# Softmax of the first cross attention: eight short exponentials on ScalarE for half of the heads

## The chip, the cores and the metric

The kernel runs on one core of a Trainium2 chip. A core has five engines with instruction queues of their own: TensorE (PE; its weight loads are listed apart as PEld), VectorE (DVE), ScalarE (ACT), GpSimd (POOL) and SyncE (SP), which issues DMAs. Each queue is worked in order: an instruction that waits holds up everything behind it on its engine. The metric is the device time of one execution in microseconds (us). The kernel before took 1720.57 us, the median of nine runs between 1716.8 and 1725.27.

## The reference

A decoder of two layers on x (16 sequences of 256 rows of 256 numbers) and a context of 77 rows per sequence, all in float32. Each layer adds an attention, a cross attention and a feed-forward part, with a layer normalization ahead of each. Layer 0 has a linear attention, the cross attention that this change touches, and a mixture of 16 experts; layer 1 has a latent attention, another cross attention and a feed-forward part with simulated quantization. The part that matters:

```python
q = jnp.einsum('bfd,dnh->bfnh', query_input, wq)        # 16 heads of 16
k = jnp.einsum('btd,dnh->btnh', source_input, wk)       # 77 context rows
v = jnp.einsum('btd,dnh->btnh', source_input, wv)
q = q * HEAD_DIM ** (-0.5)
logits = jnp.einsum('btnh,bfnh->bnft', k, q) + bias
weights = jax.nn.softmax(logits, axis=-1)
attn = jnp.einsum('bnft,btnh->bfnh', weights, v)
return jnp.einsum('bfnh,nhd->bfd', attn, wo)
```

For every row of x and every one of 16 heads there is a softmax over 77 numbers: subtract the largest, exponentiate, divide by the sum.

## The kernel before

The 4096 rows of x lie in SBUF as 32 tiles of 128 rows (`E.xs`). The stages follow each other: linear attention (`l0_attention`), cross attention (`l0_cross`), experts (`l0_experts`), layer 1's two attentions (`l1_tokens`), layer 1's feed-forward (`l1_ffn`).

`l0_cross` (line 1009) goes over the 32 tiles. For tile i, `scores(i)` (line 1032) multiplies queries and keys into PSUM in two halves (m = 0 and 1) of eight heads each, `ps_sc`. For each half a DVE step adds the mask and writes `lx_s` (128 rows, 8 heads, 77 numbers: 616 per row); DVE takes the maximum of each head, `lx_mx`; POOL subtracts it (`lx_s<-lx_s,lx_mx`); ACT exponentiates all 616 in place; DVE sums each head into `lx_sum`. After both halves DVE takes the reciprocal `lx_rec` of the 16 sums and POOL spreads it to `lx_wide`. `weighted(i)` (line 1071) turns `lx_s` with 16 transposes on PE into PSUM (`ps_pt`), from where four copies bring it to `lx_sT`; PE turns `lx_wide` and multiplies the weights with the values (`ps_rec`); a copy `lx_rT` and a DVE product `lx_aT` apply the reciprocal; PE multiplies with the output weights, and DVE adds the result to x. `scores(i + 1)` is recorded ahead of `weighted(i)`, so the softmax of one tile has the products of the tile before beside it. PSUM banks for transposes, projections and router products come from one ring of three (`pp`), `ps_rec` has one buffer, `lx_s` four.

Beside this loop run, for every four tiles, the queries and keys of a later group (`hT`, `lx_q`, `lx_k`, `ps_v`), and the router of the experts for the group before (`R.take`: normalization `la_rstd` on POOL, `la_shift` on DVE, `rh` on ACT, transposes `ps_rt`, products `ps_logit`, then `rt_...` steps on DVE, and eight indirect DMAs per group from POOL that scatter rows into `moe_x`). For the last tiles the router goes in smaller steps, tile by tile.

The order on each engine isn't that of the program. `planned` (class `Plan`, line 54 on) records all operations of a stage with estimated durations and lays them out one by one: among operations that can begin within 150 ns of the earliest it takes the one with the lowest rank (place in the program, shifted by `urgent`). The instructions are then issued in order of their planned begin; the profile gives nearly all of them line 363, where `Call.issue` calls the engine. A PSUM copy recorded with `copy` may go to DVE or ACT; the planner takes the one that would end it sooner. So another cost at one place changes the order, and the engine of copies, elsewhere in the stage.

Of the kernel before, what the change touches and what calls it, by code (L numbers as in the profile page):

```python
# [21 lines left out]
AF = mybir.ActivationFunctionType  # L22
ALU = mybir.AluOpType
AX = mybir.AxisListType
# [984 lines left out]
def l0_cross(E, W, X, raw, made):  # L1009
# [9 lines left out]
    with ExitStack() as ctx, planned(E) as nc:  # L1019
# [12 lines left out]
        def scores(i):  # L1032

            G, a = X.ready[i // 4], i % 4
            cols = slice(a * P, (a + 1) * P)
            sums = w3.tile([P, KD, 8], F32, name="lx_sum", tag="lx_sum")
            filled = []
            for m in range(KD):

                sc = psc.tile([P, 2, 512], F32, name="ps_sc", tag="sc")  # L1040
                with nc.together():
                    for r in range(2):
                        rows = slice(64 * r, 64 * r + 64)
                        nc.tensor.matmul(
                            sc[:, r, : Q * S2], G.qT[m][rows, cols],
                            X.keyed[i // 4][m][rows, i % 4 // 2, :, :].rearrange("p n k -> p (n k)"),
                            start=True, stop=True,
                        )
                filled.append(sc)
            weights = []  # L1050
            for m in range(KD):
                s = w3.tile([P, 8, S2], F32, name="lx_s", tag="lx_s", bufs=4)
                nc.vector.tensor_tensor(
                    s.rearrange("p (r n) k -> p r n k", r=2),
                    filled[m][:, :, : Q * S2].rearrange("p r (n k) -> p r n k", n=Q),
                    G.bias[:, a, :].unsqueeze(1).unsqueeze(1).to_broadcast([P, 2, Q, S2]),
                    ALU.add,
                )
                mx = w3.tile([P, 8, 1], F32, name="lx_mx", tag="lx_mx")
                nc.vector.tensor_reduce(mx, s, AX.X, ALU.max)  # L1060
                nc.gpsimd.tensor_tensor(s, s, mx.to_broadcast([P, 8, S2]), ALU.subtract)
                nc.scalar.activation(s, s, AF.Exp)
                nc.vector.tensor_reduce(sums[:, m, :], s, AX.X, ALU.add)
                weights.append(s)
            rec = w3.tile([P, H0], F32, name="lx_rec", tag="lx_rec")
            nc.vector.reciprocal(rec, sums.rearrange("p m n -> p (m n)"))
            wide = w3.tile([P, H0, DH0], F32, name="lx_wide", tag="lx_wide")
            nc.gpsimd.tensor_copy(wide, rec.unsqueeze(2).to_broadcast([P, H0, DH0]))
            return weights, wide
# [52 lines left out]
        def step(side, n=1):  # L1122
            for _ in range(n):
                next(side, None)

        held = scores(0)
        f = kv = route = last = none
        for i in range(NT):
# [6 lines left out]
            if i + 1 < NT:  # L1135
                held = scores(i + 1)
                mark = len(nc.ops) - 1
# [956 lines left out]
```

## Time and profile before

| what | us |
|---|---|
| median of nine runs | 1720.57 |
| profiled execution | 1722.94 |
| its span, first to last instruction | 1721.2 |
| PE busy (9268 matmuls) | 1588.3 |
| DVE busy | 1129.6 |
| ACT busy | 736.2 |
| POOL busy | 498.4 |
| first and last start of the masking step `lx_s<-ps_sc` | 275.1 and 549.2 |

The profile is of one execution. Its times count from the first instruction. "Busy" is the time in which an engine had at least one instruction under way; rows give the mean of one instruction, and instructions of a queue can overlap by some tens of nanoseconds, so the distance between two starts can be smaller than a duration. An arrow to the left names the tile or the step that something came from or waited for. The granted clock is TensorE's, as a share of full speed.

### The profile page before, as it was taken

To read this page: it belongs to the slowest core of one execution; us is meant where nothing else is said; L and a number is where in the kernel's file an instruction comes from. 1 tells how busy PE (TensorE), PEld (TensorE's weight loads), DVE (VectorE), ACT (ScalarE), POOL (GpSimd) and SP (SyncE) were. 2 spreads that over 40 slices of the span, in tenths; PEclk is the share of its full clock that TensorE was granted. 3 is DMA by queue.
4 is the path that set the end of the run, shared out by engine and by line. 5 is a ranking of instruction groups with operands and counts; after the bars stand their busy time and mean duration, and the time that the engine had idled before them with its cause. 6 is when DMAs were issued, how large, how long until landed. Compare 5 with 4: busy or idle time off the path is not lost.

```text
span 1721.2 us, 24227 instructions
## 1 busy us (share of the span) xinstructions
PE 1588.3 (92%) x9268; PEld 1067.4 (62%) x9268; DVE 1129.6 (66%) x2212; ACT 736.2 (43%) x1551; POOL 498.4 (29%) x570
## 2 busy tenths in 40 slices
PE   6999999999996799999997999999999689999799
PEld 3666666666664667777775666666666444433387
DVE  7988886999996343211123888966767543899941
ACT  4343324556563211111112654554555343667850
POOL 5332113576666200000003787433343100000000
PEclk9999999999997699999998999999999899999899
DMA  6000008211011154343322121000000000001111
GB/s 187 1 1 1 2 1 244 78 43 33 29 36 38 51 173 129 111 138 125 123 83 68 45 65 47 4 1 1 1 1 1 1 1 0 25 25 61 37 50 49
DMA packets 75231, 90.76 MB, mean 53 GB/s; under 512 B 11934, under 2 KB 64886, under 8 KB 75114
## 3 DMA queue, kind: packets, MB, share of 16 engines
q1 hardware_dynamic: 68970, 72.64, 13.1%
q0 software_dynamic: 6144, 16.57, 3.0%
q8 instruction: 73, 1.20, 0.3%
q14 instruction: 44, 0.36, 0.1%
HBM read 52.70 MB, written 36.70 MB: 52 GB/s over the span
## 4 chain that ended last, share of the span: by engine, by line
PE 59%; DVE 25%; issue 6%; ACT 5%; DMA 2%; POOL 1%; SPq 1%; POOLq 0%; ACTq 0%; DVEq 0%
PE ps_y L363 7%; PE ps_h L363 7%; PE ps_pr L363 7%; PE ps_av L363 5%; PE ps_out L486 5%; PE ps_gate L486 5%; PE ps_sc L363 4%; PE ps_pt L363 4%; PE ps_v L363 2%; PE ps_po L363 2%; DVE sa_top L363 2%; DVE lx_s L363 2%; PE ps_rec L363 2%; DVE x L363 2%; DVE ff_g L1957 2%
## 5 line engine op out<-in xcount | busy, mean ns | idle before, releaser
L363 DVE COPY ex_y<-ps_y 128x256 f32<-128x256 f32 x80 | 33.7, 424 | 218.7 <-PE ps_y L363 218.7
L363 POOL DMA_INDIRECT ex_yg<-moe_y,slot x64 | 63.4, 991 | 347.2 <-issue 345.7
L363 POOL TENSOR_TENSOR sa_e<-sa_e,sa_rec 128x1024 f32<-128x1024 f32 x64 | 121.5, 1905 | 121.2 <-PE ps_pt L363 71.4
L486 PE MATMUL ps_up<-ff_x,ffn_up 128*128 128x512 f32 x336 | 148.7, 601 | 7.1 <-DVE ff_pu L1828 4.3
L363 ACT ACTIVATE sa_e<-ps_sc,sa_top 128x256 f32<-128x256 f32 x256 | 118.2, 485 | 72.4 <-DVE sa_top L363 70.1
L363 PE MATMUL ps_y<-w,ex_h 128*128 128x256 f32 x640 | 143.2, 383 | 3.8 <-DVE ex_y L363 3.8
L363 PE MATMUL ps_h<-ex_xT,w 128*128 128x320 f32 x512 | 143.9, 439 | 0.5 <-ACT ex_h L363 0.5
L363 PEld LDWEIGHTS ps_y<-w,ex_h 128*128 128x128 f32 x640 | 122.5, 192 | 23.6 <-DVE ex_y L363 5.0
L363 ACT ACTIVATE ex_h<-ps_h 128x640 f32<-128x640 f32 x64 | 45.0, 704 | 186.9 <-PE ps_h L363 186.9
L363 PEld LDWEIGHTS ps_h<-ex_xT,w 128*128 128x128 f32 x512 | 96.9, 192 | 40.6 <-issue 1.2
L486 PEld LDWEIGHTS ps_up<-ff_x,ffn_up 128*128 128x128 f32 x336 | 63.6, 192 | 92.1 <-issue 74.5
L486 PE MATMUL ps_out<-ffn_down,ff_g 128*128 128x256 f32 x384 | 85.8, 388 | 10.3 <-issue 10.3
L486 PE MATMUL ps_gate<-ff_x,ffn_gate 128*128 128x512 f32 x192 | 84.2, 601 | 6.5 <-DVE ff_x L1930 6.5
L486 PEld LDWEIGHTS ps_out<-ffn_down,ff_g 128*128 128x128 f32 x384 | 74.8, 195 | 21.8 <-issue 11.1
L363 DVE TENSOR_REDUCE sa_top<-ps_sc 128x4 f32<-128x1024 f32 x64 | 76.3, 1214 | 16.4 <-PE ps_sc L363 15.9
L363 POOL TENSOR_TENSOR lx_s<-lx_s,lx_mx 128x616 f32<-128x616 f32 x64 | 77.8, 1221 | 25.4 <-DVE lx_mx L363 14.7
L363 DVE TENSOR_TENSOR la_at<-ps_sc,la_tri 128x1024 f32<-128x1024 f32 x64 | 75.8, 1214 | 8.6 <-PE ps_sc L363 8.6
L363 PE MATMUL ps_pt<-ident,lx_s 128*77 128x128 f32 x512 | 77.5, 295 | 0.4 <-ACT lx_sT L363 0.4
L363 ACT COPY lx_sT<-ps_pt 77x512 f32<-77x512 f32 x113 | 62.0, 582 | 30.5 <-PE ps_pt L363 29.4
L363 POOL DMA_INDIRECT moe_x<-rh,slot x64 | 64.7, 1011 | 31.1 <-issue 10.5
L363 PE MATMUL ps_pt<-ident,sa_e 128*128 128x128 f32 x512 | 67.3, 283 | 6.1 <-DVE x L363 1.9
L363 PE MATMUL ps_sc<-sa_latT,sa_q 64*128 64x256 f32 x512 | 70.1, 400 | 2.3 <-ACT sa_e L363 2.3
(289 smaller groups left out, 3377.7 us busy)
## 6 DMA issues: line engine op xcount, KB each, us to landing
w<-in_L_ffn_w SPq DMA_DIRECT2D x32, 512.0 KB, 3.8
moe_x<-rt_zero SPq DMA_DIRECT2D x16, 640.0 KB, 8.2
ex_xg<-moe_x SPq DMA_DIRECT2D x15, 640.0 KB, 6.7
moe_y<-ex_y SPq DMA_DIRECT2D x15, 640.0 KB, 5.7
x<-in_x SPq DMA_DIRECT2D x32, 128.0 KB, 3.3
out_x<-x SPq DMA_DIRECT2D x32, 128.0 KB, 1.7
ff_u<-ff_c SPq DMA_DIRECT2D x6, 512.0 KB, 2.9
ff_c<-ff_u SPq DMA_DIRECT2D x6, 512.0 KB, 3.2
```

Source lines behind the costliest of these rows:

```text
L363: made = getattr(getattr(self.nc, self.engine), self.method)(*self.args, **self.kwargs)
L486: E.nc.tensor.matmul(ps, a, b, start=n == 0, stop=n == last)
L1957: nc.vector.scalar_tensor_tensor(gp, low16(gq, I16), sg16, low16(sig, U16), ALU.mult, ALU.mult)
```

## The change

For the second half of each tile (m = 1) the maximum is taken with its sign turned, and instead of one subtraction on POOL, one exponential on ACT and one sum on DVE there are eight activations on ACT, one per head of 77 numbers. Each adds the negative maximum as its bias, exponentiates in place, and gives the head's sum into `lx_sum` through the activation's accumulator. The first half (m = 0) is as before. `weights.append(s)` moves up so that both halves reach it.

```diff
                 mx = w3.tile([P, 8, 1], F32, name="lx_mx", tag="lx_mx")
+                weights.append(s)
+
+
+                if m:
+                    nc.vector.tensor_reduce(mx, s, AX.X, ALU.max, negate=True)
+                    for n in range(8):
+                        nc.scalar.activation(
+                            s[:, n, :], s[:, n, :], AF.Exp, bias=mx[:, n, :],
+                            accum_out=sums[:, m, n : n + 1],
+                        )
+                    continue
                 nc.vector.tensor_reduce(mx, s, AX.X, ALU.max)
                 nc.gpsimd.tensor_tensor(s, s, mx.to_broadcast([P, 8, S2]), ALU.subtract)
                 nc.scalar.activation(s, s, AF.Exp)
                 nc.vector.tensor_reduce(sums[:, m, :], s, AX.X, ALU.add)
-                weights.append(s)
```

The planner's estimate for an activation is 170 ns and 0.73 ns per number, and 92 ns more with an accumulator (line 347).

## The prediction

> **What bounds the kernel now.** I read the page first: TensorE (PE) is busy 92% of the span, VectorE (DVE) 66%, ScalarE (ACT) 43%, GpSimd (POOL) 29%. The changed stage, cross attention of layer 0, shows in the instruction rows as the stretch from 275 to about 580 us (first and last `lx_s` work). So the second view is the table of windows over that stretch. Columns: window length, then busy us and instruction count of PE, PE's weight loads, DVE, ACT and POOL, then granted clock, DMA share, GB/s.
>
> ```profile
> 345.00:381.00 36.00, 34.00 (x311) 24.22 (x310) 34.21 (x93) 21.19 (x41) 24.37 (x31) 1.00 0.13 42
> 381.00:416.00 35.00, 33.59 (x306) 23.74 (x305) 33.20 (x91) 21.28 (x41) 22.51 (x30) 1.00 0.10 33
> 416.00:452.00 36.00, 34.59 (x313) 24.51 (x312) 34.20 (x94) 21.28 (x41) 23.50 (x30) 1.00 0.12 38
> 452.00:487.00 35.00, 33.53 (x306) 23.81 (x306) 33.20 (x90) 21.27 (x41) 22.54 (x30) 1.00 0.10 32
> 487.00:523.00 36.00, 33.33 (x306) 23.29 (x304) 33.09 (x83) 20.80 (x39) 23.29 (x30) 1.00 0.10 34
> 523.00:560.00 37.00, 22.47 (x161) 17.88 (x161) 22.61 (x62) 13.67 (x26) 21.26 (x29) 0.66 0.10 36
> ```
>
> The reader is to see two engines full at once: in the five steady windows (178 us) PE is busy 169.0 us and DVE 167.9 us, both some 95%, ACT 59%, POOL 65%. The work repeats every 35.44 us, four tiles of 128 rows (the same DVE step starts at 400.13 and 435.57). Only in the last window does everything thin out, with the clock at 0.66. Third, the waits between 275 and 556 us:
>
> ```profile
> ACT lx_rT L363 <- PE ps_rec L363: 28.3, 25, 2.0
> POOL lx_wide L363 <- DVE lx_rec L363: 25.0, 13, 3.1
> ACT lx_s L363 <- POOL lx_s L363: 24.4, 27, 3.4
> PEld ps_rec L363 <- DVE lx_aT L363: 20.0, 26, 2.6
> POOL lx_s L363 <- DVE lx_mx L363: 14.7, 19, 1.9
> PE ps_rec L363 <- DVE lx_aT L363: 10.0, 15, 2.3
> ```
>
> (us in all, times, longest.) ACT and POOL wait for the full engines. PE itself has only one large wait, the output product behind `lx_aT`, 10.0 us. PE hardly ever waits for an exponential: its transposes of `lx_s` lost 0.4 us in all (that row reads "ACT lx_sT"). The three-engine softmax is hidden one tile ahead.
>
> **The change, priced.** Of 64 half tiles, 32 take the new form. The operations that go, and the one row of the same shape as the one that comes (the last layer's `cx_s`, ACT, in order of time):
>
> ```profile
> L363 DVE TENSOR_REDUCE lx_sum<-lx_s x64: 761/787/796, 281.8 to 554.2; 128x8 f32<-128x616 f32 x64
> L363 POOL TENSOR_TENSOR lx_s<-lx_s,lx_mx x64: 1207/1217/1254, 276.8 to 552.2; 128x616 f32<-128x616 f32 x64
> L363 ACT ACTIVATE lx_s<-lx_s x64: 700/717/736, 278.0 to 553.5; 128x616 f32<-128x616 f32 x64
> ```
> ```profile
> 1024.90 0.36 ACT L363 ACTIVATE cx_s<-cx_s,cx_top 128x77 f32<-128x77 f32 x1 [3.18 <-DVE cx_top L363]
> 1025.16 0.19 ACT L363 ACTIVATION_READ_ACCUMULATOR cx_s<-cx_s,cx_top 128x1 f32 x1
> 1025.26 0.34 ACT L363 ACTIVATE cx_s<-cx_s,cx_top 128x77 f32<-128x77 f32 x1
> ```
>
> Consecutive starts in the trace of before are closer than durations: 0.34 us per head with its accumulator read inside, 0.63 for the wide exponential, 0.71 for a DVE reduction, 0.60 and 0.49 for a 77x512 copy on DVE and ACT. I count in these.
>
> *ACT.* 256 heads x 0.342 = 87.6, plus 32 x 0.09 for the last read of a burst = 2.9; less 32 x 0.63 = 20.2.
>
> *What moves.* The planner chooses the engine of every PSUM copy by when ACT and DVE come free, so a fuller ACT sheds copies. The built order of the changed kernel shows it: on DVE `lx_sT` copies go from 15 to 38, `hT` from 9 to 20, `lx_rT` from 0 to 4, `rhT` from 3 to 4. Off ACT go 23 x 0.49 + 11 x 0.49 + 4 x 0.29 + 0.49 = 18.3. ACT gains 87.6 + 2.9 - 20.2 - 18.3 = 52 us on its 157 in 275-556.
>
> *DVE.* 32 x 0.71 = 22.7 go; 23 x 0.60 + 11 x 0.60 + 4 x 0.33 + 0.6 = 22.3 come. So DVE, one of the two full engines, is relieved by 0.4 us in all. In a steady group it is 4 x 0.71 - (1 + 2) x 0.60 - 0.33 = 0.7 us less; the last group takes it back in copies. This is the heart of my forecast: the balance undoes the relief.
>
> *POOL.* 32 x 1.22 = 39 us go. POOL is not full; its worth is indirect. First, at some places a DVE step stretches under a POOL subtraction:
>
> ```profile
> 544.96 1.35 DVE L363 TENSOR_TENSOR wgt<-rt_top,rt_both 128x8 f32<-128x8 f32 x1
> 545.05 1.23 POOL L363 TENSOR_TENSOR lx_s<-lx_s,lx_mx 128x616 f32<-128x616 f32 x1
> ```
>
> Its median is 0.166. Seven `wgt` at a mean of 0.403, seven `rt_both` at 0.363 against 0.155, seven `rt_valid` at 0.271 against 0.17 make 1.7 + 1.5 + 0.7 = 3.9 us of stretch. Half the subtractions gone: between 0 and 3.9, I take 1. The Trainium skill, SBUF — State Buffer, section "SBUF: two separate sides", has the rule: VectorE with two SBUF inputs and GpSimd take a shared port pair as an exclusive lock, and the loser blocks for the whole instruction. By it all stretched steps whose covering subtraction is gone would be cured, so about half of 3.9, 2 us; it makes no other term.
>
> *The chain of one half.* Maximum to last head exponential: before 1.22 + 0.1 + 0.72 = 2.04 (POOL, handoff, ACT); after 8 x 0.342 = 2.74. To the finished sums: before 2.04 + 0.1 + 0.79 = 2.93; after 2.83. In the steady groups one tile of lookahead (8.9 us) hides both. If that cover were gone, the transposes would be 0.7 us late per tile, 22 us over 32 tiles; PE's 0.4 us of wait there says it is not near.
>
> *The tail,* where nothing hides it. PE sits idle from 550.50 to 556.03, waiting for the router's `rh` on ACT (555.38), which waits for `la_shift` on DVE (555.24), queued behind the sum of the last half (554.24), which waits for the subtraction on POOL (552.22-553.46) behind two indirect DMAs. After: two DVE sums (0.71 each) are gone between 547.98 and 552, one `lx_rT` copy (0.33) comes; the last maximum ends near 550.4 instead of 551.7. Then ACT does one head, the wide exponential and seven heads, 0.34 + 0.63 + 2.39 + 0.1 handoff = 3.5, to 553.9, and `rh` follows: 1.5 us earlier. What is late next is ACT's burst itself, no longer POOL. The earlier gap is the same in both:
>
> ```profile
> 522.06 0.44 PE L363 MATMUL ps_rec<-ident,lx_wide 128*128 128x128 f32 x2
> 527.29 2.16 PE L363 MATMUL ps_rt<-ident,rh 128*128 128x128 f32 x8 [4.79 <-ACT rh L363]
> 529.91 3.60 PE L363 MATMUL ps_logit<-w_L_ffn_gate_wT,rhT 128*128 128x16 f32 x16 [0.46 <-ACT rhT L363]
> ```
>
> There `rh` stands behind the burst (exponential to 523.0, heads to 525.8) instead of `la_rstd` behind POOL; `la_shift` is ready near 526.0 instead of 526.25. Worth 0.2. After such gaps the clock is down: the 16 small matmuls take 3.60 us, in the steady groups 1.85. The Trainium skill, TensorE: Matmul & The Clock Gate, Part 1, says that about 3.4 us of idling halves the clock and about 3.4 us of work restores it. The 4.8 us gap with its slow matmuls agrees; by the page the gap at 550.5, 5.5 shortened to 4.0, still pays, so it adds nothing to my sum.
>
> *Steady groups.* DVE's 0.7 us per group, 3.5 us over five. PE's idle there is 178 - 169 = 9 us, so that caps any gain; between 0 and 3.5 I take 2.5, since `lx_aT`, PE's largest wait, is itself a DVE step.
>
> *Queueing on ACT.* Each burst (2.83 us) now stands in one queue with the copies that PE waits for. Behind a burst directly stand, in the built order, 5 `lx_rT` copies (`lx_aT` and PE's output product wait for them), 13 `lx_sT` copies (a PSUM bank is held), and in two cases `rh`. ACT had 124 us idle and `lx_rT` mostly found it waiting (28.3 us); now it has 72 idle. Bounds: 0 if each burst fits the idle; 18 x 1.4 (half a burst) = 25 if each is met in its middle and PE has nothing else. I take 1.2, near the low end, because the copies that would meet bursts were moved to DVE.
>
> No DMA is moved; SP's order is the same. POOL's indirect DMAs come earlier, if at all.
>
> Sum: -1.0 (POOL) -1.5 -0.2 (tail) -2.5 (steady) +1.2 (ACT queue) = -4.0 us. The profiled execution took 1722.94 us (span 1721.2), 2.4 above the median of nine, 1720.57. So 1718.9 on its own scale, **1716.6 us** on the median's. About 0.2% (3.4 us) is what a measurement here can tell from no change.
>
> **Rivals.** *A: ACT's queue becomes the bound (slower).* For: ACT rises from 21.3 to 28.3 us of 35.44 in a group, with three engines between 80 and 96% and only three PSUM buffers between them; a copy one burst late stops PE in order. Against: PE runs at 95% with ACT at 59% and its copies are shared. Price: half of the above bound, 12 us on the median, to 1732; it decides once more than three or four of the 18 copies lose their 1.4 us on PE's path.
> *B: PE is not really full (faster).* Its weight loads are busy only 24 of 36 us per window, so matmul time might hold slack, and POOL's hop leaves a loop that could tighten. Against: back-to-back runs start without gaps (ps_sc x4 every 0.72 us). Price: PE's idle of 9 steady plus 6.1 in 275-345 plus 2 in the tail, two thirds of it: -11, to 1709.5.
> *C: nothing to see.* DVE's load is unchanged and PE's work is the same; gains and losses of one or two us cancel: 1719 to 1722.
>
> **How the numbers follow.** Main case, a gain of 2 to 7 us: 0.42. A: 0.36. B: 0.12. C: 0.10. The main case's own range is 1713.5 to 1718.5. Faster by over 0.2% (below 1717.1): about two thirds of the main case, 0.28, and B, 0.12: 0.40. Slower by over 0.2% (above 1724): A but for its mildest end, 0.34. Within: the rest, 0.26. The range leaves out the far ends of A and B, one in ten each: 1707.5 to 1731.
>
> **What would show it.** ACT about 28 us busy per 35 us, heads at 0.34; DVE still 33 of 35; POOL some 39 us less; the period near 35.0; `rh` after the last half 1.5 us earlier. A period above 35.8, or PE waits on ACT's `lx_sT` or on `lx_aT` beyond 15 us, would show A and make me wrong; a period under 34.3 shows B.

## The result and the profile after

The changed kernel took 1733.45 us (median of 13 runs, 1727.93 to 1736.15) against 1720.81 for the kernel before beside it: a ratio of 1.0067, 95% interval 1.0057 to 1.0078, so it is slower by 11.5 us by the ratio (the two medians alone lie 12.6 us apart). Two more sets gave 1.0068 (1.0047 to 1.0089) and 1.0064 (1.0047 to 1.0081). The forecast, 1716.6 us, had the wrong sign, and the time lies beyond the range.

The table of windows of the changed kernel, in the stretches shown of before (columns as there):

```profile
345.00:381.00 36.00, 33.81 (x308) 24.21 (x308) 34.09 (x95) 26.44 (x94) 15.99 (x25) 1.00 0.08 27
381.00:416.00 35.00, 32.56 (x298) 22.93 (x294) 33.54 (x95) 25.70 (x93) 16.59 (x24) 1.00 0.11 36
416.00:452.00 36.00, 33.26 (x280) 23.53 (x276) 33.36 (x91) 27.16 (x97) 16.90 (x25) 1.00 0.10 32
452.00:487.00 35.00, 33.07 (x300) 23.30 (x299) 30.77 (x82) 25.04 (x94) 16.64 (x24) 1.00 0.10 32
487.00:523.00 36.00, 33.57 (x301) 23.64 (x300) 30.14 (x77) 25.55 (x94) 17.05 (x24) 0.95 0.09 31
523.00:560.00 37.00, 27.84 (x254) 20.80 (x250) 26.48 (x69) 19.36 (x69) 18.70 (x26) 0.85 0.12 44
```

ACT rose from 21.2 to about 26 us per window and POOL fell from 23.2 to 16.6. Over the whole run ACT is busy 44.6 us longer (52 forecast), POOL 39.2 us less (39 forecast) and DVE 1.0 us longer (0.4 less forecast). PE, which should have become denser, is busy 166.3 us of the 178 in the first five windows, after 169.0. The groups of four tiles are longer. I measure them from one first `ps_rank` product to the next: before, 37.6, 35.5, 35.4, 35.4, 33.3 us; after, 39.5, 36.8, 36.7, 38.2, 36.0. That is 9.8 us over five groups: PE is idle 6.7 us longer in them (14.2 after 7.5) and busy 3.1 us longer (172.9 after 169.8) with the same products, and DVE's busy time rises from 166.8 to 170.1. From 518 us on the new kernel is faster by 1.4 us in all, and before the first group slower by 1.3: at the end of the stage it stands 9.7 us behind.

The instruction rows, and the waits in the changed stage (275 to 566 us):

```profile
L363 ACT ACTIVATE lx_s<-lx_s,lx_mx x256: 342/345/364, 279.1 to 564.2; 128x77 f32<-128x77 f32 x128
L363 ACT ACTIVATION_READ_ACCUMULATOR lx_s<-lx_s,lx_mx x256: 185/188/200, 279.3 to 564.4; 128x1 f32 x128
L363 POOL TENSOR_TENSOR lx_s<-lx_s,lx_mx x32: 1214/1217/1233, 277.5 to 560.2; 128x616 f32<-128x616 f32 x32
L363 ACT ACTIVATE lx_s<-lx_s x32: 700/717/731, 281.1 to 561.5; 128x616 f32<-128x616 f32 x32
L363 DVE TENSOR_REDUCE lx_sum<-lx_s x32: 775/788/796, 282.0 to 562.2; 128x8 f32<-128x616 f32 x32
```
```profile
POOL lx_wide L363 <- DVE lx_rec L363: 46.1, 11, 5.9
...
ACT lx_s L363 <- POOL lx_s L363: 19.7, 18, 2.6
...
ACT lx_rT L363 <- PE ps_rec L363: 18.0, 15, 1.6
PEld ps_rec L363 <- DVE lx_aT L363: 17.3, 24, 2.7
ACT lx_s L363 <- DVE lx_mx L363: 15.7, 12, 3.7
...
PE ps_rt L363 <- ACT rh L363: 11.2, 13, 4.1
```

The operations are what the forecast said they would be, down to the price of a head. No single wait of PE grew by the 10 us that are lost: its wait for `lx_aT` is 8.3 us (10.0 before), for `rh` 11.2 (10.3 before, but in 13 pieces, not 2), for the masked scores 4.7 (3.1 before). POOL's wait for `lx_rec` grew from 25.0 to 46.1, with 39 us less work on POOL. New is that ACT stands 15.7 us before a head, waiting for DVE's maximum. The tail came out as forecast: the two long waits for `rh` shrank from 4.79 and 5.53 us to

```profile
538.41 1.95 PE L363 MATMUL ps_rt<-ident,rh 128*128 128x128 f32 x7 [3.99 <-ACT rh L363]
541.03 3.59 PE L363 MATMUL ps_logit<-w_L_ffn_gate_wT,rhT 128*128 128x16 f32 x16 [0.46 <-ACT rhT L363]
565.15 1.18 PE L363 MATMUL ps_rt<-ident,rh 128*128 128x128 f32 x4 [4.12 <-ACT rh L363]
```

and after the gap the small products still take 3.6 us.

One place per group caught my eye first. In the changed kernel's timeline of PE the output product stands between the two `ps_rank` products, and waits:

```profile
407.49 0.33 PE L363 MATMUL ps_rank<-rt_hits,rt_before 128*128 128x64 f32 x2
408.79 1.13 PE L363 MATMUL ps_rec<-w_L_xattn_wo,lx_aT 128*128 128x256 f32 x4 [0.97 <-DVE lx_aT L363]
409.75 0.33 PE L363 MATMUL ps_rank<-rt_cum,rt_ones 128*128 128x64 f32 x2
```

where before it had

```profile
403.11 0.33 PE L363 MATMUL ps_rank<-rt_hits,rt_before 128*128 128x64 f32 x2
403.28 0.39 PE L363 MATMUL ps_rank<-rt_cum,rt_ones 128*128 128x64 f32 x2
```

and ACT's timeline one group later shows why `lx_aT` is late: a lone head that waits for its maximum stands in front of the copy into `lx_rT`, whose operand was there at 443.3:

```profile
444.63 0.36 ACT L363 ACTIVATE lx_s<-lx_s,lx_mx 128x77 f32<-128x77 f32 x1 [1.68 <-DVE lx_mx L363]
...
444.98 0.35 ACT L363 COPY lx_rT<-ps_rec 128x256 f32<-128x256 f32 x1
```

So I began with three theories: ORDER, that such places cost the time; LOAD, that 52 us more on ACT in blocks of 2.7 us do; REPLAN, that the newly laid order with its copies moved to DVE does.

### The profile page after: what moved, and what is told of

Same layout as the page of the kernel before. It is cut to its first block, busy times and chain, and to the rows that moved or that the text cites. A ratio compares the mean times of both kernels' runs of the same rounds, so it can differ in the third digit from the quotient of the medians.

```text
span 1732.0 us, 24621 instructions
## 1 busy us (share of the span) xinstructions
PE 1594.3 (92%) x9268; PEld 1070.1 (62%) x9268; DVE 1130.6 (65%) x2219; ACT 780.8 (45%) x1992; POOL 459.2 (27%) x538
## 4 chain that ended last, share of the span: by engine, by line
PE 58%; DVE 23%; issue 7%; ACT 6%; POOL 3%; DMA 2%; SPq 1%; POOLq 0%; ACTq 0%; DVEq 0%
PE ps_y L363 7%; PE ps_h L363 7%; PE ps_pr L363 6%; PE ps_av L363 5%; PE ps_out L486 5%; PE ps_gate L486 5%; PE ps_pt L363 4%; PE ps_sc L363 4%; PE ps_v L363 3%; PE ps_po L363 2%; DVE x L363 2%; DVE sa_top L363 2%; DVE ff_g L1967 2%; PE ps_rec L363 2%; ACT lx_s L363 2%
## 5 line engine op out<-in xcount | busy, mean ns | idle before, releaser
L486 PE MATMUL ps_out<-ffn_down,ff_g 128*128 128x256 f32 x384 | 85.8, 387 | 10.3 <-issue 10.3
L363 ACT ACTIVATE lx_s<-lx_s,lx_mx 128x77 f32<-128x77 f32 x256 | 88.0, 347 | 15.7 <-DVE lx_mx L363 15.7
L486 PEld LDWEIGHTS ps_out<-ffn_down,ff_g 128*128 128x128 f32 x384 | 74.7, 195 | 21.8 <-issue 11.1
L363 PEld LDWEIGHTS ps_pt<-ident,lx_s 128*77 128x77 f32 x512 | 63.8, 160 | 15.3 <-issue 3.8
```

Source lines behind the costliest of these rows:

```text
L363: made = getattr(getattr(self.nc, self.engine), self.method)(*self.args, **self.kwargs)
L486: E.nc.tensor.matmul(ps, a, b, start=n == 0, stop=n == last)
```

## The experiments

The sets ran at two speeds: the kernel before took 1723.3 and 1723.5 us in the second and fourth set, 1736.5, 1737.6 and 1737.4 in the first, third and fifth, which I call the slower sets. Whether the chip makes the difference isn't shown: the first set carries the same chip number, 6, as the second and fourth. Every ratio is against the kernel before of its own set; I compare kernels across the two kinds of set with care, for a reason that comes out at the end. The changed kernel itself was never run in a slower set.

**First set: four ways to place the heads (slower set).**

*Heads as one operation.* `with nc.together():` around the eight activations, with the planner's duration of such an operation set to their sum.

> The changed kernel, with the eight heads of a tile entered in the issue order as one operation, so that no copy can stand between two heads, or behind a single head that waits for its maximum; the planner also lays its copies anew. Theory ORDER (a lone head that waits for VectorE's maximum, or a burst of heads, stands in ScalarE's queue ahead of the copy into lx_rT, and TensorE's next product gets its operand 1.0 to 1.3 us late in each group): the lone heads are gone, so the five steady groups (from one group's first ps_rank product to the next one's) come back from a mean of 37.4 us to 36.5 or less, and the time to 1723 to 1729. Theory LOAD (the 52 to 70 us that ScalarE has more to do in blocks of 2.8 us cost the time, wherever the copies stand): no recovery, 1732 to 1738, since what arrives during a burst now waits for all of it. Theory REPLAN (it is the copies that the planner put on VectorE that cost): here it puts 45 of the lx_sT copies there in place of 38, so 1733 or more.

Ratio 1.0084 (1.0061 to 1.0108), beside 1.0067 for the changed kernel in a faster set: no recovery to be seen.

*The old order.* Every operation is planned as before; where it is issued, the second half's is replaced:

```diff
-nc.gpsimd.tensor_tensor(s, s, mx.to_broadcast([P, 8, S2]), ALU.subtract)
-nc.scalar.activation(s, s, AF.Exp)
-nc.vector.tensor_reduce(sums[:, m, :], s, AX.X, ALU.add)
+nc.gpsimd.tensor_tensor(..., ALU.subtract, instead=skip)
+nc.scalar.activation(s, s, AF.Exp, instead=heads)
+nc.vector.tensor_reduce(..., ALU.add, instead=skip)
```

> The changed kernel's operations at the places where the kernel before has theirs: order and engine of every other instruction as before, the eight heads where the second half's wide exponential stood, GpSimd's subtraction and VectorE's sum of the second half left out at theirs. The lx_sT copies on VectorE are 15 as before, not 38, and none of the lx_rT copies is there. Theory REPLAN (the newly laid order, with 23 lx_sT copies and 4 lx_rT copies more on VectorE, costs the time): recovered, 1715 to 1722. Theory LOAD: ScalarE now carries the heads and all its copies, some 22 us more than in the changed kernel, so 1735 to 1745. Theory ORDER: twelve lx_rT copies stand right behind a burst; each that waits for it is up to 2.8 us late, so 1728 to 1740, with TensorE's waits for lx_aT above those of the kernel before.

Ratio 1.0123 (1.0104 to 1.0142). The recovery that REPLAN expected did not come. The old order does not suit the blocks: PE waits 23.8 us for `lx_aT` over the whole run, against 10.4 in the first trace of before; a part of this comes from the late starts told of with the last kernel.

*`lx_rT` on VectorE.* `nc.copy(rT, pr[:, D:])` becomes `nc.vector.tensor_copy(rT, pr[:, D:])`.

> The changed kernel with every copy into lx_rT on VectorE (32 in place of 4), so that no lx_rT stands behind a head on ScalarE. Theory ORDER: TensorE's waits for lx_aT in the steady groups shrink by 1 us a group and the time comes back to 1724 to 1729. Theory LOAD: ScalarE is relieved of 28 copies of 0.25 us, 7 us of its 52, so a gain of 1 to 2 us at most: 1731 to 1734. Theory REPLAN: VectorE carries some 7 us more, so 1733 to 1738.

Ratio 1.0098 (1.0082 to 1.0114). The wait is still there; it moved to DVE's queue, where the copy now stands behind a sum:

```profile
414.65 0.78 DVE L363 TENSOR_REDUCE lx_sum<-lx_s 128x8 f32<-128x616 f32 x1
415.35 0.41 DVE L363 COPY lx_rT<-ps_rec 128x256 f32<-128x256 f32 x1
```
```profile
416.28 1.13 PE L363 MATMUL ps_rec<-w_L_xattn_wo,lx_aT 128*128 128x256 f32 x4 [1.03 <-DVE lx_aT L363]
```

*Heads without the rest.* In the kernel before, the second half's exponential is cut into eight plain ones.

> The kernel before with the second half's wide exponential cut into eight of one head each, without bias and without accumulated sums: GpSimd's subtraction and VectorE's sum of the second half stay. So ScalarE gets nearly all of the changed kernel's load and VectorE and GpSimd no relief. Theory LOAD: at least as slow as the changed kernel, 1732 to 1742, as the relief is lacking too. Theory ORDER: the heads wait for GpSimd's subtraction, not for the maximum, and the copies stand where the planner lays them against that; 1722 to 1730. Theory REPLAN: few copies can go to a VectorE that still has its sums, so near the kernel before plus what those cost, 1721 to 1728.

Ratio 1.0117 (1.0099 to 1.0135). As slow as LOAD expected, and yet the load is hardly there: without accumulators eight heads take 1.37 us, and ACT is busy 749 us in all, 13 more than before, where the changed kernel has 45 more. The relief is lacking too, so this alone refutes nothing, but it speaks for the order that the planner lays around the eight operations. None of the three theories gave all four results: REPLAN missed the old order and this kernel, LOAD missed `lx_rT` on VectorE, and ORDER missed all but the old order.

**Second set: the dose (at the first measurement's speed).** The kernel before once more gave 1.0010 (0.9997 to 1.0023), so 0.1 to 0.2% is what these comparisons resolve, and its groups came out as in the first trace within 0.1 us.

> The kernel before once more, for a trace from the same chip as the other kernels of this set. Every theory expects a ratio of 1.000 (within 0.2%), and steady groups of 35.4 us.

The changed kernel once more: 1.0068.

> The changed kernel once more, beside the others of this set. Every theory expects the ratio measured first, 1.0067, within 0.2%; if it comes out at 1.009 or more, the cost of the change depends on the chip, and the differences of 0.2 to 0.3% between this kernel and the ones with the heads as one operation or with lx_rT on VectorE were the chip's.

Half the dose, `if m and i % 2:` in place of `if m:`

> The changed form on the odd tiles alone: 16 half tiles and 128 heads in place of 32 and 256. Theory LOAD (cost in proportion to ScalarE's added time, +26 us in place of +52): half of the changed kernel's loss, a ratio of 1.003 to 1.004. Theory FIT (any tile whose softmax gets a longer block on ScalarE opens a gap in TensorE's order, and a gap of about 1.1 us or more also brings a spell of half clock that costs 1.7 us; the relief on VectorE gives part of it back): the router's heavy tiles decide and not the count, so anything from 1.001 to 1.007, with the loss in whole steps in some groups and none in others. Theory REPLAN: fewer copies move to VectorE, 1.000 to 1.002.

and twice the dose, `if True:`

> The changed form for both halves of every tile: 512 heads, no subtraction on GpSimd and no sum on VectorE is left in this stage. Theory LOAD: ScalarE gains some 100 us net of the copies that leave it and is busy over 33 of some 40 us per group, so it is the bound: ratio 1.015 to 1.03. Theory FIT: gaps in every tile, but VectorE is relieved of 45 us: 1.008 to 1.02. Theory REPLAN: 75 of the lx_sT copies go to VectorE, whose relief they take back: 1.005 to 1.012.

They gave 1.0080 (1.0062 to 1.0099) and 1.0078 (1.0058 to 1.0099). With 128, 256 and 512 heads the loss is the same within the intervals. In the kernel with 512, ACT is busy 32.3 of 36.9 us per group, and its middle groups are no longer than those of the changed kernel. LOAD, a cost in proportion to the heads (1.003 to 1.004 for the half, 1.015 to 1.03 for the double), falls. But each dose also brought a relief and an order of its own, so this does not show that heads cost nothing.

**Third set: other orders (slower set).** The planner's margin of 150 ns is set to another value for this stage, `nc.near = 140`, with no other edit.

> The kernel before with its operations unchanged, planned anew: the margin by which the planner of this stage lets a more urgent operation wait (150 ns) is 140 ns, so only the order of the instructions and the engine of some copies differ. Theory LOTTERY (the kernel before has an order that happens to fit, all three middle groups alike with 1.1 us of TensorE waits each, and nearly any other order costs gaps and, with them, spells of half clock): 1.003 to 1.010, as the kernels with 128, 256 and 512 heads, which all lay at 1.007 to 1.008. Theory HEADS (the blocks of heads on ScalarE cost the time, whatever their number): 0.998 to 1.002, as no heads are here.

> The same with a margin of 160 ns: a second new order of the kernel before's own operations. Theory LOTTERY: 1.003 to 1.010. Theory HEADS: 0.998 to 1.002. If this one loses and the one at 140 ns does not, the scatter between orders is about as large as the change's effect, and the change cannot be told from it.

> The same with a margin of 130 ns, a third order, in which TensorE changes less often between products of different shapes. Theory LOTTERY: no order is good by itself, 1.000 to 1.010. Theory HEADS: 0.998 to 1.002. If TensorE's own work bounds the groups and this order spares it changes of shape, it can be below 1: 0.993 to 0.999.

> The changed kernel planned with a margin of 130 ns. Beside the kernel before at 130 ns it gives the effect of the change under another order. Theory HEADS: the same loss as at 150 ns, 0.6 to 0.8% above the kernel before at 130 ns. Theory LOTTERY: the difference between these two is anything from -0.3% to +0.8% and need not have the sign that it has at 150 ns.

The kernel before gave 1.0009 (0.9996 to 1.0023) at 140, 1.0034 (1.0021 to 1.0048) at 160 and 1.0009 (0.9998 to 1.0021) at 130; the changed kernel at 130 gave 1.0023 (1.0011 to 1.0035). So new orders of the old operations lose at most 0.3%, two of the three nothing that could be told from noise, less than I gave them. But the change, which costs 0.67% at 150 in the faster sets, costs 0.14% at 130 here (1.0023 - 1.0009, give or take 0.17).

**Fourth set: order and block taken apart (at the first measurement's speed).**

> The changed kernel, for the same chip as the other three. Every theory expects 1.007 within 0.2%; if a ratio near 1.002 comes out, the kernel at a margin of 130 ns owed its small loss to its chip and not to its order.

> The changed kernel's operations, all 256 heads among them, in the order that the planner lays with a margin of 130 ns. Theory ORDER-FIT (the loss comes from how the planned order fits the block, so another order of the same operations loses less): 1.001 to 1.004, clearly below the changed kernel beside it. Theory BLOCK (2.7 us of heads in ScalarE's queue cost the same in any order): 1.006 to 1.008, like it.

Then two kernels with the same operations in the two orders: the second half has neither subtraction nor sum, and one exponential of all 616 columns, 0.63 us, in place of 2.7 us of heads. In the changed kernel's order:

```diff
 for n in range(8):
     nc.scalar.activation(
         s[:, n, :], s[:, n, :], AF.Exp, bias=mx[:, n, :],
-        accum_out=sums[:, m, n : n + 1],
+        accum_out=sums[:, m, n : n + 1], instead=skip if n else once,
     )
```

> The changed kernel's order and choice of engines, instruction by instruction, but where the first of the eight heads stands, one exponential of all 616 columns (0.63 us, shifted by the first head's maximum, no accumulated sums) takes the place of the eight (2.7 us); the second half is divided by the first half's sums, so this part of the result is left out. Theory BLOCK: with the block gone and the relief on VectorE and GpSimd kept, at or below the kernel before, 0.992 to 1.000, and TensorE's waits for lx_aT and rh fall below those of the kernel before. Theory ORDER (the newly laid order costs by itself, with its 23 lx_sT copies moved to VectorE): still 1.003 to 1.007.

and in the order of the kernel before, with the same three replacements as in the first set and `heads` now this one exponential:

> The same operations as in the kernel with the one short exponential, but in the order of the kernel before: the second half's subtraction on GpSimd and sum on VectorE are left out at their places, the wide exponential stands where it stood, shifted by the first head's maximum; the second half is divided by the first half's sums, so this part of the result is left out. It shows what the relief is worth without any block: bounded by the 1.1 us a group that TensorE waits, 0.995 to 0.999 in theory BLOCK and in theory ORDER alike. If it is 1.000 or more, there was nothing to be gained from the relief at all, and the steady groups' gain in the forecast was empty. Beside the kernel with the short exponential it gives the price of the new order alone.

| kernel | order laid for | block on ACT | ratio, 95% interval |
|---|---|---|---|
| changed | heads, margin 150 | 2.7 us | 1.0064 (1.0047 to 1.0081) |
| changed, margin 130 | heads, margin 130 | 2.7 us | 1.0007 (0.9996 to 1.0018) |
| one exponential | heads, margin 150 | 0.63 us | 1.0058 (1.0038 to 1.0078) |
| one exponential | before | 0.63 us | 0.9936 (0.9919 to 0.9954) |

This settles the main question for these two orders. With the block gone and the order kept, the loss stays (third row); with the block kept and the order changed, the loss is gone (second row), though the relief brings no gain there either. And the same operations in the old order are 1.22% faster than in the new one, 21 us, give or take 5 (rows three and four); the last row gained more than both theories had expected (0.995 at best). The busy times of the whole run, in the new and then the old order:

```profile
PE 1598.9 (92%) x9268; PEld 1073.7 (62%) x9268; DVE 1131.8 (65%) x2219; ACT 719.2 (41%) x1512; POOL 458.7 (26%) x538
PE 1587.9 (93%) x9268; PEld 1068.1 (62%) x9268; DVE 1105.3 (65%) x2180; ACT 736.6 (43%) x1551; POOL 460.6 (27%) x538
```

With the moved copies on it, DVE is busy 26.5 us longer in the new order. PE is busy 11.0 us longer with the same 9268 products, of 23.6 us between the two spans (1736.9 and 1713.3). Much of that is the clock: from 345 to 356 us and from 509 to 517 us the kernel in the new order has a granted clock of 0.53 and 0.57, which makes some 17 us at half speed and an estimated 8.6 us lost; the one in the old order has 1.00 from 345 to 356 and from 501 to 517. So in the five groups the order costs PE 11.1 us of idle time (15.0 against 3.9) and 10.0 us of busy time (177.9 against 167.8). That both leave out a part of the result does not bear on this: behind the stage, from the last `ps_rank` pair to the end, they take 1133.7 and 1135.9 us, the kernel before 1133.8 and the changed one 1134.9.

The eight heads do not fit the old order any better: with them it gave 1.0123 in the first set, with one exponential 0.9936 here. That is some 32 us between the two, an estimate across the two kinds of set; 10.1 us of it are late starts, as counted below. So a block costs 1 us in the order that the planner laid for it and much more in the old one: the loss belongs to order and blocks together.

The table of windows, group by group: the kernel with one exponential in the new order,

```profile
376.29:413.17 36.88, 34.20 (x310) 24.41 (x309) 34.82 (x97) 19.58 (x37) 17.85 (x25) 1.00 0.11 34
413.17:450.16 36.99, 34.19 (x310) 24.41 (x309) 35.06 (x96) 19.68 (x37) 17.92 (x25) 1.00 0.11 34
```

in the old order,

```profile
365.75:400.19 34.44, 33.59 (x309) 24.14 (x308) 31.14 (x88) 21.19 (x41) 18.18 (x26) 1.00 0.11 36
400.19:434.63 34.44, 33.59 (x310) 24.14 (x309) 31.13 (x88) 21.19 (x41) 18.15 (x26) 1.00 0.11 37
```

and the changed kernel's operations, blocks and all, at margin 130:

```profile
408.64:444.18 35.54, 33.67 (x310) 24.05 (x309) 30.92 (x84) 26.61 (x98) 17.22 (x24) 1.00 0.11 36
444.18:479.75 35.57, 33.68 (x309) 24.05 (x308) 29.63 (x80) 26.59 (x98) 16.70 (x23) 1.00 0.11 36
```

PE does the same 309 or 310 products in each. In the old order DVE has 3.7 us less to do per group than in the new one and the group is 2.4 us shorter. In the new order DVE has 96 instructions instead of 88 in these groups; that it has no reserve left and so holds up PE is argued, not shown. How many copies moved to DVE does not decide by itself: at margin 130 the built order has 41 `lx_sT` copies there, three more than at 150, and loses nothing. What these two groups at margin 130 have in common with the old order is that DVE is busy 31 us or less, and that the two `ps_rank` products stand together; the group ahead of them, with 36.3 us of DVE, took 36.9 us there too.

**Fifth set: the place, and the relief (slower set).** From the changed kernel's planned order I moved six instructions by one place.

> The changed kernel with six instructions moved by one place, two in each of three groups (those that begin at 370.7, 407.5 and 444.2 us in the changed kernel's trace): on TensorE the second ps_rank product goes ahead of the output product that waits for lx_aT; on ScalarE the lone head that waits for VectorE's maximum goes behind the copy into lx_rT. Theory PLACE (these two places hold the group up: TensorE waits 1.0 to 1.3 us there, and the expert's slots, and with them the run of scatters on GpSimd and the next rh, come 1.6 us later than in the kernel before): the three groups come down from 36.8, 36.7 and 38.2 us by 1.0 to 1.6 us each, 3 to 5 us in all, ratio 1.0035 to 1.005. Theory SPREAD (the new order loses a little at many places, and what is mended here is lost at the next one): the waits move on, less than 1.5 us is won, 1.006 to 1.007.

Ratio 1.0097 (1.0077 to 1.0116): nothing won that could be seen. The timelines of PE and then of DVE in the middle of the three groups:

```profile
411.07 0.33 PE L381 MATMUL ps_rank<-rt_hits,rt_before 128*128 128x64 f32 x2
411.24 0.39 PE L381 MATMUL ps_rank<-rt_cum,rt_ones 128*128 128x64 f32 x2
412.28 1.13 PE L381 MATMUL ps_rec<-w_L_xattn_wo,lx_aT 128*128 128x256 f32 x4 [0.65 <-DVE lx_aT L381]
```
```profile
411.81 0.42 DVE L381 TENSOR_TENSOR lx_aT<-ps_rec,lx_rT 128x256 f32<-128x256 f32 x1
...
413.79 0.28 DVE L381 TENSOR_TENSOR rt_hot<-rt_hot,ps_rank 128x128 f32<-128x128 f32 x1
```

The second `ps_rank` product now ends at 411.6, and the DVE step that uses it still starts at 413.79, behind normalizations in DVE's queue; `lx_rT` was copied at 410.25, and `lx_aT` still starts at 411.81. PE's wait only shrank from 0.97 to 0.65 us. The wait moved on to DVE, as SPREAD has it. The ratio itself can't decide between PLACE and SPREAD, because the changed kernel as it is was not run in this set.

The last kernel was meant to beat both: the old order, and no shift in the softmax at all.

> The kernel before in its own order, with the maximum (VectorE) and the subtraction (GpSimd) left out at their places in both halves of every tile; the wide exponentials and the sums stay. A softmax is the same without the shift as long as the scores are below some 88 and no row is masked altogether, which holds for these inputs. No blocks, no new order, and twice the relief of the kernel with the second half's subtraction and sum left out (0.9936). If the relief keeps paying: 0.985 to 0.990. If TensorE is the bound once 1 us a group is won: 0.990 to 0.9945. Above 0.996 the gain measured there did not come from the relief.

Ratio 1.0029 (1.0015 to 1.0044), though DVE is relieved by 49 us and POOL by 78. By what I had written, that would mean that the gain of the kernel with one exponential did not come from the relief. But its timelines of PE and ACT show where the time went, once per group:

```profile
369.01 1.08 PE L367 MATMUL ps_rec<-lx_sT,lx_v 77*32 77x128 f32 x32
...
374.83 2.08 PE L367 MATMUL ps_rec<-w_L_xattn_wo,lx_aT 128*128 128x256 f32 x4 [3.50 <-DVE lx_aT L367]
```
```profile
373.95 0.37 ACT L367 COPY lx_rT<-ps_rec 128x256 f32<-128x256 f32 x1 [5.39 <-remote]
```

The product that the copy needs ended at 370.09; ACT had nothing else to do and began 3.9 us later, put down to a releaser that the trace does not know. Counted over all traces (copies into `lx_rT` that start over 0.3 us after their product's end, with the engine idle for over 0.5 us): none in any of the ten traces from the first measurement and the second and fourth set, and 5 to 10 in each of the ten from the slower sets, 4.8 to 21.2 us in all; 21.2 in this kernel, 13.2, 13.6 and 15.9 in the three other orders of the kernel before. One kernel was traced at both speeds, the changed one at margin 130: no such copy and a span of 1719.8 us in the fourth set, 7 of them with 16.7 us and a span of 1742.6 in the third. So the late starts come with the set and not with the order. Results of the slower sets carry such a term, of a size that differs from kernel to kernel, and what this kernel's relief is worth stays open. Whether this kernel would beat the kernel before at the faster speed was not tried. No kernel that I ran and that computes the whole result beats the kernel before; the changed one at margin 130 cannot be told from it in the faster sets.

## Why the prediction failed

- **"The balance undoes the relief."** The step that failed. I counted the copies that the planner moves, priced them on DVE, and took the newly laid order as neutral otherwise. In busy time over the whole run the balance held (DVE +1.0 us). In the five groups it did not: I had 0.7 us less per group, and DVE's busy time rose by 0.7 us per group. Above all, order and relief are not worth what the balance of busy times says. With the old order, and one exponential for the heads, the relief is worth 0.64%, 11 us, 5.5 of them in the five groups, where I capped it at 3.5; each middle group falls from 35.44 to 34.44 us and PE's wait for `lx_aT` in the stage from 10.0 to 5.2 us. Whether DVE's own load or the shorter chain over POOL, ACT and DVE brings this was not separated. And the new order, with its moved copies, costs 1.22%, 21 us, where my sum let the copies cancel the relief and put the order at nothing. -11, +21 and +1 for the blocks give the 11 measured because each is measured from the one before; by way of the blocks in the old order the parts would have other sizes.
- **"Steady groups", -2.5.** Measured +9.8 over five groups. This is where the failed step shows.
- **"Queueing on ACT", +1.2.** The size fits, for the order that was laid: from one short exponential to eight heads in that order the time goes from 1.0058 to 1.0064, 1 us, give or take 4.5, which cannot tell 1.2 from nothing. The reason, that the planner lays the copies so that blocks do not hurt, agrees with the old order's loss under blocks (1.0123); that laying was the dear part.
- **Rival A**, 1732 us, has the measured time but not the cause. One of its signs (a period above 35.8) appeared, the other (PE waits beyond 15 us for `lx_aT`) did not, at 8.3 us. As the cause of this loss its mechanism (a burst that holds up PE's copies) is refuted by the kernel without bursts in the same order, which is as slow; in the old order, where PE waits 23.8 us for `lx_aT`, it may well be at work. A right price with a wrong mechanism would have led to the wrong mend.
- **Tail**, -1.5 and -0.2: right in sum. The stretch with the last two full router steps gives 2.0 us back, 0.6 of which is lost again later; `rh` stands right behind ACT's last head, as forecast.
- **POOL's stretch of DVE**, -1.0: hardly came: counted as in the prediction, 3.4 us of the 3.9 us of stretch are still there. `wgt` is cured (its longest is 0.168 us, 1.353 before), but `rt_both` now falls under a subtraction in the steady groups. DVE and POOL:

```profile
441.30 0.92 DVE L363 TENSOR_TENSOR rt_both<-rt_top 128x4 f32<-128x4 f32 x1
```
```profile
440.98 1.22 POOL L363 TENSOR_TENSOR lx_s<-lx_s,lx_mx 128x616 f32<-128x616 f32 x1 [0.71 <-PE ps_pt L363]
```

The Trainium skill, SBUF — State Buffer, section "SBUF: two separate sides", says that the loser of the shared port blocks for the whole of the other's instruction; `rt_both`, 0.156 us by its median, ends here within 0.02 us of the subtraction. The rule agrees; which step falls under which subtraction is once more a matter of the order.

What stays open: which single decision of the planner starts the loss. The two kernels with one exponential differ at nearly every group, by 2.4 to 7.2 us, so it is spread; whether it comes from DVE's fuller queue or from the order on PE was not separated, and neither was how much of it another execution would lose to the lowered clock.

## What to carry to other kernels

Where a planner lays the queues, an edit has two effects: its own, and that of the order laid anew; the second can be the larger one (here 21 us against a relief of 11). They can be looked at apart, by issuing the new operations at the old places and cheap stand-ins at the new ones, and it pays to do this before explaining the loss by the new operations. The prices so found hold for the path taken, since an order is laid for its operations. When halving and doubling a change gives the same loss, a cost in proportion to its work is not the cause.

## What was not expected of the hardware

- In these traces spells of half clock last whole multiples of 3.4 us, and one followed gaps of 1.1 us or less. PE's timeline and the windows of the changed kernel:

```profile
502.16 1.91 PE L363 MATMUL ps_rt<-ident,rh 128*128 128x128 f32 x8 [1.09 <-ACT rh L363]
```
```profile
500.00:502.00 2.00, 0.66 (x4) 1.00 0.00 0
502.00:504.00 2.00, 1.67 (x8) 1.00 0.00 0
504.00:505.00 1.00, 1.00 (x25) 0.63 0.00 0
505.00:506.00 1.00, 1.00 (x17) 0.50 0.00 0
506.00:507.00 1.00, 1.00 (x2) 0.50 0.00 0
507.00:508.00 1.00, 1.00 (x3) 0.66 0.00 0
```

The columns are length, PE's busy time and count, granted clock, DMA share, GB/s. Gaps of 0.54 and 1.09 us within 2.3 us were followed by about 3.4 us at half clock, which costs 1.7 us; a single gap of 2.23 us at 344.8 had no such spell. The kernel before has none in its steady groups. The Trainium skill, TensorE: Matmul & The Clock Gate, Part 1, speaks of an idle window of about 3.4 us; no gap of that length stands ahead of this spell. As the longer gap had no spell and the shorter ones had, the length of a gap alone does not decide, nor does a threshold of about 1.1 us as the expectation with the odd tiles had it; what does is not shown.
- Exponentials of 77 columns with a bias and accumulated sums start every 0.342 us, plain ones every 0.16: bias and accumulator together cost more than the exponential. The bias has a share in it: in the kernels of the fourth set with one exponential of 616 columns, it takes 0.81 us with a bias and 0.72 without.
- In the slower sets copies start up to microseconds after their operand is ready (above); the kernel before is 14 us slower there, about what these late starts add up to in its other orders, 13 to 16 us. That they are the reason is not shown, nor what holds the copies back.
